# Masked attention layer on one core: eleven exponential tiles, the mask in 1 KB pieces, and exponentials issued behind the value products

## The chip, the cores and the metric

The kernel runs on one core of a Trainium2 chip. The metric is the device time of the whole program in microseconds (us): 3736.42 us for the kernel before, the median of three runs (3731.55 to 3740.82).

A core has five engines that run side by side and wait for each other through semaphores: TensorE (PE in the profile; its weight loads are PEld), VectorE (DVE), ScalarE (ACT), GpSimd (POOL), and SyncE (SP), which here only issues transfers. Each engine works through its own queue of instructions. Transfers run on 16 DMA engines. Matrix products are written to PSUM, which has eight banks; everything else lives in SBUF, with 128 partitions.

## What is computed

One graph-attention layer over 8 batch entries of 2048 nodes with 256 channels and 8 heads of 32, with one adjacency matrix for all of them:

```python
qkv = jnp.einsum('fnc,ck->fnk', x, w_qkv)          # q, k, v: (F, N, H, D) each, F=8, N=2048, H=8, D=32
scores = jnp.einsum('fnhd,fmhd->fhnm', q, k) / jnp.sqrt(D)
scores = jnp.where((adj > 0)[None, None, :, :], scores, -1e9)
attn = jax.nn.softmax(scores, axis=-1)
t = jnp.einsum('fhnm,fmhd->fnhd', attn, v).reshape(F, N, C)
x1 = _layernorm(x + t, ln1_g, ln1_b)
h = jax.nn.relu(jnp.einsum('fnc,cd->fnd', x1, w1) + b1)
f_out = jnp.einsum('fnd,dc->fnc', h, w2) + b2
x2 = _layernorm(x1 + f_out, ln2_g, ln2_b)
return _layernorm(x + x2)                          # without weights
```

About one adjacency entry in 128 is set, but the kernel computes all scores and masks them.

## The kernel before

The work is cut into 1024 steps. A step `(f, qc, g, mb)` is one batch entry `f`, one quarter `qc` of the queries (512), one half `g` of the heads (4 heads) and one of 16 blocks `mb` of 128 keys. Sixteen steps with the same `(f, qc, g)` are called a group here, and a group with `g = 1` an odd one; an entry has eight groups.

The scores of a step lie in PSUM with the keys on the partitions. VectorE adds the mask (0, or -57344 where there is no edge) on the way to SBUF, in two halves, and ScalarE takes the exponential in place. The mask is kept as 8-bit floats, keys on the partitions, 8 KB per partition for a query quarter; two such tiles rotate.

```python
mkp = ctx.enter_context(tc.tile_pool(name="mkp", bufs=2))
ld = ctx.enter_context(tc.tile_pool(name="ld", bufs=LD))     # LD = 3 tiles for loads ("in")
pp = ctx.enter_context(tc.tile_pool(name="pp", bufs=10))     # "p": scores and exponentials, 8 KB per partition
...
def scores(item):
    f, qc, g, mb = item
    pt = PT[item] = pp.tile([P, 4, CH], F32, name="p")
    ps2 = [score_pair() for _ in range(2)]                   # two of three pairs of PSUM banks
    for half in (1, 0):
        for j in range(2):
            r = D * (2 * half + j)
            nc.tensor.matmul(ps2[half][:, j, :], KT[...][r:r + D, ...], QT[f, qc, g][r:r + D, :], start=True, stop=True)   # L223
    for half, ps in enumerate(ps2):
        nc.vector.tensor_tensor(pt[:, 2 * half:2 * half + 2, :], ps,
                                MK[f, qc][:, mb, None, :].to_broadcast([P, 2, CH]), ALU.add)      # L226
    nc.scalar.activation(pt, pt, AF.Exp, scale=1.0 / math.sqrt(D))                                # L228

def values(item):
    f, qc, g, mb = item
    if mb == 0:
        O[grp] = ps_x[state["side"]].tile(...)               # one of two PSUM banks, in turn by group
    for h in range(4):
        nc.tensor.matmul(O[grp][r:r + D, :], V[...], PT[item][:, h, :], start=(mb == 0), stop=(mb == LAST))   # L240
    if mb == LAST:
        OT[grp] = op.tile([P, CH], F32, name=f"oT{g}")
        nc.scalar.copy(OT[grp], O.pop(grp))                  # L244, frees the bank
```

The softmax's denominators need the sum of the 16 exponential tiles of a group. Two chains of four are added by DMA, one chain of seven on GpSimd, one tile is left alone, and the four sums go through TensorE at the group's end. A `p` tile is free again only when its sum is done:

```python
POOLED = (0, 3, 6, 8, 11, 13, 15)
MOVED = ((1, 4, 7, 10), (2, 5, 9, 12))
def add_up(item):
    for chain in MOVED:
        if mb in chain[1:]:
            nc.gpsimd.dma_start(PT[f, qc, g, chain[0]], PT.pop(item), accum_op=ALU.add)           # L257
    if mb in POOLED[1:]:
        nc.gpsimd.tensor_tensor(first, first, PT.pop(item), ALU.add)                              # L260
```

All other work (denominators, normalizations, the two dense layers, projections of the next entry, masks of the next quarter) is cut into small pieces that the program places between the steps, one PSUM bank's worth per step, in the bank that the current group doesn't use:

```python
LEAD = 2
for t, (f, qc, g, mb) in enumerate(items):
    if mb == 0 and t:
        state["side"] = 1 - state["side"]
    if f == 0 and g == 0 and mb == 0 and qc + 1 < NCK:
        start(t, mask_ahead(qc + 1), t + 28)
    if g == 1 and mb == 0 and (f or qc == NCK - 1) and ...:
        load_mask(f + (qc + 1) // NCK, (qc + 1) % NCK)
    ...
    if mb:
        advance(t, 1)                   # a piece of other work
    scores(items[t + LEAD])             # scores, mask and exponential of two steps ahead
    values(items[t])
    add_up(items[t])
```

The mask is made once, in the first entry: adjacency rows are loaded, VectorE turns them to 0 or -57344, TensorE transposes them, VectorE writes them as 8-bit floats, and the quarter goes to DRAM for the seven later entries. The first quarter is made before the first step, in four blocks; the others are made between the steps, four blocks `mc` each:

```python
def turn_mask(qc, mc):
    if mc == 0:
        MK[0, qc] = mkp.tile([P, MB, CH], F8, name="mask")
    yield INPUTS - 3                    # needs all three "in" tiles
    cv = take([P, TPC, CH], BF16)
    ts = [take([P, 2, CH], I32) for _ in range(2)]
    for half, t in enumerate(ts):
        nc.sync.dma_start(t, adj[...])                                                            # L121
        nc.vector.tensor_scalar(cv[:, 2 * half:2 * half + 2, :], t, 0.0, MASKED, op0=ALU.is_le, op1=ALU.mult)   # L122
        give(t)
        yield 1                         # go on a step later
    yield 1
    yield from mask_blocks(qc, mc, cv)  # two halves: 8 transposes (L136) and one minimum (L137) each
    give(cv)                            # after the last block of a quarter: MD[qc] <- MK[0, qc] (L140)

def begin():
    ...                                 # loads; first quarter of the mask; keys and values for g = 0
    for k in range(LEAD):
        scores(items[k])
    for c in range(NCK):
        yield from project(0, c, 1, rows[c][:, 2:4, :])      # keys and values for g = 1
```

Of the kernel before, what the change touches and what calls it, by code (L numbers as in the profile page):

```python
# [10 lines left out]
F32 = mybir.dt.float32  # L11
BF16 = mybir.dt.bfloat16
I32 = mybir.dt.int32
F8 = mybir.dt.float8e5
# [4 lines left out]
P = 128  # L19
H = 8  # L20
D = 32
# [32 lines left out]
def fast_path(ctx, tc, cst, x, adj, out, RS):  # L54
# [3 lines left out]

    LD = 3
    dp = ctx.enter_context(tc.tile_pool(name="dp", bufs=1, space=bass.MemoryType.DRAM))  # L60
    mkp = ctx.enter_context(tc.tile_pool(name="mkp", bufs=2))
    ld = ctx.enter_context(tc.tile_pool(name="ld", bufs=LD))
    kp = ctx.enter_context(tc.tile_pool(name="kp", bufs=2 * NCK + 2))
    qp = ctx.enter_context(tc.tile_pool(name="qp", bufs=2 * NCK + 2))
    vp = ctx.enter_context(tc.tile_pool(name="vp", bufs=2 * NCK + 2))
    pp = ctx.enter_context(tc.tile_pool(name="pp", bufs=10))
    work = ctx.enter_context(tc.tile_pool(name="work", bufs=1))
    yp = ctx.enter_context(tc.tile_pool(name="yp", bufs=2))
    op = ctx.enter_context(tc.tile_pool(name="op", bufs=1))
# [33 lines left out]
    def give(t):  # L103
        live[:] = [None if u is t else u for u in live]


    MD = dp.tile([NCK, P, MB * CH // 4], I32, name="md")
    MK = {}

    def words(mask):  # L110
        return mask.rearrange("p b q -> p (b q)").bitcast(I32)

    def turn_mask(qc, mc):
        if mc == 0:
            MK[0, qc] = mkp.tile([P, MB, CH], F8, name="mask")
        yield INPUTS - 3
        cv = take([P, TPC, CH], BF16)
        ts = [take([P, 2, CH], I32) for _ in range(2)]
        for half, t in enumerate(ts):
            q0 = qc * CH + half * 2 * P  # L120
            nc.sync.dma_start(t, adj[q0:q0 + 2 * P, mc * CH:(mc + 1) * CH].rearrange("(j p) m -> p j m", p=P))  # L121
            nc.vector.tensor_scalar(cv[:, 2 * half:2 * half + 2, :], t, 0.0, MASKED, op0=ALU.is_le, op1=ALU.mult)  # L122
            give(t)
            yield 1
        yield 1
        yield from mask_blocks(qc, mc, cv)
        give(cv)

    def mask_blocks(qc, mc, cv):
        for half in range(2):  # L130
            yield BANK
            ps = bank(BF16)
            for r in range(2):
                for j in range(TPC):
                    rr = 2 * half + r
                    nc.tensor.transpose(ps[:, r, j * P:(j + 1) * P], cv[:, j, rr * P:(rr + 1) * P], identb)  # L136
            nc.vector.tensor_tensor(MK[0, qc][:, mc * TPC + 2 * half:mc * TPC + 2 * half + 2, :], ps,  # L137
                                    cst["ones"][:, 0:1, None].to_broadcast([P, 2, CH]), ALU.min, saturate=False)
        if mc == NCK - 1:
            nc.sync.dma_start(MD[qc], words(MK[0, qc]))  # L140

    def load_mask(f, qc):
        MK[f, qc] = mkp.tile([P, MB, CH], F8, name="mask")
        nc.sync.dma_start(words(MK[f, qc]), MD[qc])


    QT, KT, V, XT = {}, {}, {}, {}
# [46 lines left out]
    def project(f, c, g, xT=None):  # L194
        if xT is None:
            xT = yield from reload(f, c)
            while len(KT) < (2 * f + g) * NCK + c:
                yield 1
        yield BANK
        KT[f, c, g] = channels(kp, "kT", xT, C + g * P)  # L200
        yield BANK
        ps = bank()
        for j in range(TPC):
            for a in range(2):
                nc.tensor.matmul(ps[:, j * P:(j + 1) * P], xT[:, a, j * P:(j + 1) * P],  # L205
                                 wqkv[:, a, 2 * C + g * P:2 * C + (g + 1) * P], start=(a == 0), stop=(a == 1))
        v = vp.tile([P, TPC, P], F32, name="v")
        nc.scalar.copy(v, ps.rearrange("p (j c) -> p j c", c=P))
        V[f, c, g] = v
        give(xT)  # L210
# [4 lines left out]
# [3 lines that stand above are left out]
        ps2 = [score_pair() for _ in range(2)]  # L218
# [4 lines that stand above are left out]
                nc.tensor.matmul(ps2[half][:, j, :], KT[f, mb // TPC, g][r:r + D, (mb % TPC) * P:(mb % TPC + 1) * P],  # L223
                                 QT[f, qc, g][r:r + D, :], start=True, stop=True)
        for half, ps in enumerate(ps2):
            nc.vector.tensor_tensor(pt[:, 2 * half:2 * half + 2, :], ps,  # L226
                                    MK[f, qc][:, mb, None, :].to_broadcast([P, 2, CH]), ALU.add)
        nc.scalar.activation(pt, pt, AF.Exp, scale=1.0 / math.sqrt(D))  # L228

    LAST = MB - 1  # L230

    def values(item):
        f, qc, g, mb = item
        grp = (f, qc, g)
        if mb == 0:
            i = state["side"]
            O[grp] = ps_x[i].tile([P, CH], F32, name=f"x{i}")
        for h in range(4):
            r = D * h
            nc.tensor.matmul(O[grp][r:r + D, :], V[f, mb // TPC, g][:, mb % TPC, r:r + D], PT[item][:, h, :],  # L240
                             start=(mb == 0), stop=(mb == LAST))
        if mb == LAST:
            OT[grp] = op.tile([P, CH], F32, name=f"oT{g}")
            nc.scalar.copy(OT[grp], O.pop(grp))  # L244
# [135 lines left out]
    def start(t, gen, due):  # L380
        fill.append([t, gen, 1, due])
        fill.sort(key=lambda e: e[3])
# [24 lines left out]
    def mask_ahead(qc):  # L407
        for mc in range(NCK):
            yield from turn_mask(qc, mc)
# [9 lines left out]
    def begin():  # L419
        flat = [pp.tile([P, 4, CH], F32, name="p").rearrange("p a q -> p (a q)") for _ in range(NCK + NCK // 2)]  # L420
        cols = [t.bitcast(I32).rearrange("p (j m) -> p j m", m=CH) for t in flat[:NCK]]
        cv = [t[:, i * 2 * CH:(i + 1) * 2 * CH].bitcast(BF16).rearrange("p (j m) -> p j m", m=CH)
              for t in flat[NCK:] for i in range(2)]
        rows = [pp.tile([P, 4, CH], F32, name="p") for _ in range(NCK)]
        for c in range(NCK):
            xc = rows[c][:, 0:2, :].rearrange("p a (b c) -> p (a b) c", c=C)
            nc.sync.dma_start(xc, x[0, c * CH:(c + 1) * CH, :].rearrange("(j p) c -> p j c", p=P))
            nc.sync.dma_start(cols[c], adj[0:CH, c * CH:(c + 1) * CH].rearrange("(j p) m -> p j m", p=P))
        MK[0, 0] = mkp.tile([P, MB, CH], F8, name="mask")
        for c in range(NCK):  # L430
            nc.vector.tensor_scalar(cv[c], cols[c], 0.0, MASKED, op0=ALU.is_le, op1=ALU.mult)
            xT = rows[c][:, 2:4, :]
            yield from turn_rows(rows[c][:, 0:2, :].rearrange("p a (b c) -> p (a b) c", c=C), xT)
            nc.sync.dma_start(XD[0][c], xT)
            XT[0, c] = xT
            if c == 0:
                yield from queries(0, 0, xT)
            yield from project(0, c, 0, xT)
            yield from mask_blocks(0, c, cv[c])
        for k in range(LEAD):  # L440
            scores(items[k])
        for c in range(NCK):
            yield from project(0, c, 1, rows[c][:, 2:4, :])

    def ask(f, c):
        xT = yield from reload(f, c)
        yield from queries(f, c, xT)
        give(xT)
# [2 lines left out]
        pass  # L451
    for c in range(1, NCK):
        start(0, ask(0, c), 2 * MB * c - LEAD - 1)
    state["side"] = 0
    for t, (f, qc, g, mb) in enumerate(items):
        if mb == 0 and t:
            state["side"] = 1 - state["side"]
        if f == 0 and g == 0 and mb == 0 and qc + 1 < NCK:
            start(t, mask_ahead(qc + 1), t + 28)
        if g == 1 and mb == 0 and (f or qc == NCK - 1) and (f + 1 < F or qc + 1 < NCK):  # L460
            load_mask(f + (qc + 1) // NCK, (qc + 1) % NCK)
        if f + 1 < F:
            for what, *which in NEXT.get((2 * qc + g, mb), []):
                due = t + MB // 2 if what is turn else items.index((f + 1, 0, which[1], which[0] * TPC)) - LEAD - 1
                start(t, what(f + 1, *which), due)
        if mb:
            advance(t, 1)
        if t + LEAD < len(items):
            nf, _, ng, nmb = items[t + LEAD]
            t0 = t  # L470
            while (nf, nmb // TPC, ng) not in V:
                advance(t0, 1)
                t0 += 1
            scores(items[t + LEAD])
        values(items[t])
        add_up(items[t])
        if mb == LAST:
            start(t + SUM, denominator(f, qc, g), t)
# [240 lines left out]
```

## Time and profile before

| | |
|---|---|
| median of three runs | 3736.42 us |
| span of the profiled execution | 3732.1 us |
| mean granted TensorE clock | 0.977 of full |
| bytes moved by DMA | 573.31 MB |
| `mask<-md`: loads of a mask quarter | 28 of 1024 KB, median 6.6 us to landing |
| `in<-in_adj_dram`: loads of adjacency rows in the loop | 24 of 512 KB, median 7.6 us to landing |
| `p<-p`: sums by DMA | 384 of 1024 KB, median 9.7 us to landing |

A group's row in the profile names the line of the kernel, the engine, the operation and its tiles, and then the count, the busy time and the mean duration in nanoseconds; behind the second bar stands how long the engine had been idle just before such instructions, and what released it. A busy share is an average over the run: the engine with the highest is not necessarily what each stretch waits for. A row of the timeline gives the start, the duration, the instruction, and in brackets the idle time before it with its releaser. The first entry runs from about 42 to 564 us, counted by its exponentials.

### The profile page before, as it was taken

To read this page: it belongs to the slowest core of one execution; us is meant where nothing else is said; L and a number is where in the kernel's file an instruction comes from. 1 tells how busy PE (TensorE), PEld (TensorE's weight loads), DVE (VectorE), ACT (ScalarE), POOL (GpSimd) and SP (SyncE) were. 2 spreads that over 40 slices of the span, in tenths; PEclk is the share of its full clock that TensorE was granted. 3 is DMA by queue.
4 is the path that set the end of the run, shared out by engine and by line. 5 is a ranking of instruction groups with operands and counts; after the bars stand their busy time and mean duration, and the time that the engine had idled before them with its cause. 6 is when DMAs were issued, how large, how long until landed. Compare 5 with 4: busy or idle time off the path is not lost. (4 is left out here: it accounts for less than half of the span.)

```text
span 3732.1 us, 53786 instructions
## 1 busy us (share of the span) xinstructions
PE 3241.8 (87%) x22020; PEld 1038.8 (28%) x22020; DVE 2760.8 (74%) x3203; ACT 2411.0 (65%) x1921; POOL 2599.1 (70%) x1363
## 2 busy tenths in 40 slices
PE   7877888899988899889998899889898889988884
PEld 4222223222322233222332223222232222322221
DVE  4777766877688766788677777777768877688883
ACT  3554555766667666766666776666666676677663
POOL 2555666777677775877667785777777777687775
PEclk9998999999999999999999999999999999999997
DMA  6766675776766775776766776676676676676664
GB/s 185 175 142 152 146 175 117 168 162 142 173 150 145 158 171 145 169 153 154 169 138 151 163 172 158 140 165 154 147 175 141 148 171 152 154 164 140 139 134 86
DMA packets 113774, 573.31 MB, mean 154 GB/s; under 512 B 10833, under 2 KB 27729, under 8 KB 60273
## 3 DMA queue, kind: packets, MB, share of 16 engines
q0 software_dynamic: 64848, 436.90, 58.1%
q1 hardware_dynamic: 47856, 131.61, 10.0%
q8 instruction: 174, 2.85, 0.3%
q10 hardware_dynamic: 816, 1.31, 0.1%
q14 instruction: 80, 0.65, 0.0%
HBM read 129.37 MB, written 37.75 MB: 45 GB/s over the span
## 5 line engine op out<-in xcount | busy, mean ns | idle before, releaser
L226 DVE TENSOR_TENSOR p<-s,mask 128x1024 f32<-128x1024 f32 x2048 | 2410.3, 1219 | 753.8 <-PE s L223 480.0
L228 ACT ACTIVATE p<-p 128x2048 f32<-128x2048 f32 x1024 | 1957.1, 1911 | 1232.9 <-DVE p L226 916.2
L260 POOL TENSOR_TENSOR p<-p 128x2048 f32<-128x2048 f32 x384 | 1835.9, 4810 | 653.6 <-ACT p L228 645.0
L223 PE MATMUL s<-qT,kT 32*128 32x512 f32 x8192 | 1193.2, 652 | 232.5 <-DVE p L226 231.0
L240 PE MATMUL x<-p,v 128*32 128x512 f32 x8192 | 1112.2, 616 | 0.0
L257 POOL DMA_DIRECT2D p<-p x384 | 382.7, 1018 | 351.2 <-ACT p L228 138.9
L223 PEld LDWEIGHTS s<-qT,kT 32*128 32x128 f32 x8192 | 325.3, 186 | 853.6 <-DVE p L226 695.6
L240 PEld LDWEIGHTS x<-p,v 128*32 128x32 f32 x8192 | 162.3, 108 | 795.2 <-issue 645.1
L180 PE MATMUL x<-in,wqkv 128*128 128x512 f32 x472 | 234.6, 620 | 23.1 <-ACT oT L244 10.2
L278 ACT ACTIVATE y<-y,nb,rs 128x256 f32<-128x256 f32 x384 | 224.9, 589 | 38.0 <-POOL nb L275 38.0
L294 PE MATMUL x<-p,ones 128*32 128x512 f32 x2048 | 246.3, 599 | 1.8 <-DVE y L364 0.9
L267 DVE BATCH_NORM_STATS2 st<-y 128x6 f32<-128x256 f32 x384 | 160.1, 417 | 27.1 <-DMA y<-in_x_dram 27.1
L362 PE MATMUL x<-w2s,hT 128*128 128x256 f32 x512 | 127.6, 392 | 45.7 <-ACT oT L244 42.3
L352 PE MATMUL x<-turned,w1s 128*128 128x512 f32 x256 | 128.8, 626 | 20.8 <-ACT hT L353 19.5
L180 PEld LDWEIGHTS x<-in,wqkv 128*128 128x128 f32 x472 | 80.3, 190 | 186.1 <-issue 69.8
L362 PEld LDWEIGHTS x<-w2s,hT 128*128 128x128 f32 x512 | 92.1, 190 | 112.0 <-ACT oT L244 68.6
L205 PE MATMUL x<-wqkv,in 128*128 128x128 f32 x896 | 114.9, 282 | 6.4 <-ACT kT L182 6.3
L205 PEld LDWEIGHTS x<-wqkv,in 128*128 128x128 f32 x896 | 104.2, 192 | 55.0 <-ACT kT L182 34.0
L364 DVE TENSOR_TENSOR y<-x,y 128x512 f32<-128x512 f32 x64 | 44.3, 692 | 94.9 <-PE x L362 94.7
L294 PEld LDWEIGHTS x<-p,ones 128*32 128x32 f32 x2048 | 64.0, 111 | 165.8 <-issue 129.7
L272 POOL TENSOR_TENSOR rs<-rs,mhalf 128x4 f32<-128x4 f32 x96 | 99.3, 1035 | 8.0
L341 PE MATMUL x<-ident,y 128*128 128x128 f32 x256 | 48.0, 299 | 54.5 <-ACT turned L342 38.8
(87 smaller groups left out, 1427.1 us busy)
## 6 DMA issues: line engine op xcount, KB each, us to landing
p<-p POOLq DMA_DIRECT2D x384, 1024.0 KB, 9.7
y<-in_x_dram POOLq DMA_DIRECT2D x64, 512.0 KB, 6.1
in<-xd SPq DMA_DIRECT2D x59, 512.0 KB, 8.0
mask<-md SPq DMA_DIRECT2D x28, 1024.0 KB, 6.6
out_dram<-y SPq DMA_DIRECT2D x32, 512.0 KB, 3.0
in<-in_x_dram SPq DMA_DIRECT2D x28, 512.0 KB, 6.9
xd<-in SPq DMA_DIRECT2D x28, 512.0 KB, 10.0
in<-in_adj_dram SPq DMA_DIRECT2D x24, 512.0 KB, 7.6
```

Of the source, the lines that this page charges most:

```text
L180: nc.tensor.matmul(ps, wqkv[:, a, k0:k0 + P], xT[:, a, :], start=(a == 0), stop=(a == 1))
L205: nc.tensor.matmul(ps[:, j * P:(j + 1) * P], xT[:, a, j * P:(j + 1) * P], wqkv[:, a, 2 * C + g * P:2 * C + (g + 1) * P], start=(a == 0), s ...
L223: nc.tensor.matmul(ps2[half][:, j, :], KT[f, mb // TPC, g][r:r + D, (mb % TPC) * P:(mb % TPC + 1) * P], QT[f, qc, g][r:r + D, :], start=Tr ...
L226: nc.vector.tensor_tensor(pt[:, 2 * half:2 * half + 2, :], ps, MK[f, qc][:, mb, None, :].to_broadcast([P, 2, CH]), ALU.add)
L228: nc.scalar.activation(pt, pt, AF.Exp, scale=1.0 / math.sqrt(D))
L240: nc.tensor.matmul(O[grp][r:r + D, :], V[f, mb // TPC, g][:, mb % TPC, r:r + D], PT[item][:, h, :], start=(mb == 0), stop=(mb == LAST))
L257: nc.gpsimd.dma_start(PT[f, qc, g, chain[0]], PT.pop(item), accum_op=ALU.add)
L260: nc.gpsimd.tensor_tensor(first, first, PT.pop(item), ALU.add)
L267: nc.vector.bn_stats(st, t[:, j, :])
L278: nc.scalar.activation(t[:, j, :], t[:, j, :], AF.Identity, bias=nb[:, j:j + 1], scale=rs[:, j:j + 1])
L294: nc.tensor.matmul(ps[r:r + D, :], cst["ones"], term[:, h, :], start=(n == 0), stop=(n == 3))
L362: nc.tensor.matmul(ps[:, (j - jj) * C:(j - jj + 1) * C], hT[:, d, j * P:(j + 1) * P], w2s[:, d, :], start=(d == 0), stop=(d == 1))
```

## The change

Four things are changed together.

- Each quarter of the mask is kept as eight pieces of two key blocks, 1 KB per partition each, from a pool of nine pieces in place of two whole quarters. Pieces of the next quarter are loaded one by one during an odd group, each as a piece of the current quarter comes free. This gives room in SBUF.
- The room is used for an eleventh `p` tile.
- The second quarter of the mask is made at the start, with the first, in `p` tiles; the third and fourth are made in the loop, as before, but a block's adjacency rows are asked for two steps ahead of their conversion, and its masks are written into the tiles that held the rows and go to DRAM from there. In the first entry too, quarters two to four are then loaded back from DRAM.
- The exponential of a step is issued after the value products of the same turn of the loop, not right after its scores.

```diff
-    mkp = ctx.enter_context(tc.tile_pool(name="mkp", bufs=2))
+    mkp = ctx.enter_context(tc.tile_pool(name="mkp", bufs=MB // 2 + 1))
-    pp = ctx.enter_context(tc.tile_pool(name="pp", bufs=10))
+    pp = ctx.enter_context(tc.tile_pool(name="pp", bufs=11))
@@ turn_mask @@
-    MD = dp.tile([NCK, P, MB * CH // 4], I32, name="md")
+    MD = dp.tile([NCK, MB // 2, P, 2 * CH // 4], I32, name="md")
+    made, coming = set(), deque()
+    def mask_piece(t, qc, k):
+        MK[t, qc, k] = mkp.tile([P, 2, CH], F8, name="mask")
+        return MK[t, qc, k]
...
             nc.sync.dma_start(t, adj[q0:q0 + 2 * P, mc * CH:(mc + 1) * CH].rearrange("(j p) m -> p j m", p=P))
+        yield 2
+        for half, t in enumerate(ts):
             nc.vector.tensor_scalar(cv[:, 2 * half:2 * half + 2, :], t, 0.0, MASKED, op0=ALU.is_le, op1=ALU.mult)
+        yield 1
+        yield from mask_blocks(qc, mc, cv, [... the tiles ts seen as 8-bit floats ...])
+        for t in ts:
             give(t)
-            yield 1
-        yield 1
-        yield from mask_blocks(qc, mc, cv)
         give(cv)
@@ mask_blocks @@
-            nc.vector.tensor_tensor(MK[0, qc][:, mc * TPC + 2 * half:...], ps, ..., ALU.min, saturate=False)
-        if mc == NCK - 1:
-            nc.sync.dma_start(MD[qc], words(MK[0, qc]))
+            k = 2 * mc + half
+            m = to[half] if to else mask_piece(0, qc, k)
+            nc.vector.tensor_tensor(m, ps, ..., ALU.min, saturate=False)
+            nc.sync.dma_start(MD[qc, k], words(m))
+            made.add((qc, k))
+    def load_mask(f, qc, k):
+        nc.sync.dma_start(words(mask_piece(f, qc, k)), MD[qc, k])
@@ scores @@
-        nc.scalar.activation(pt, pt, AF.Exp, scale=1.0 / math.sqrt(D))
+    def exponentials(item):
+        nc.scalar.activation(PT[item], PT[item], AF.Exp, scale=1.0 / math.sqrt(D))
@@ begin @@
         for k in range(LEAD):
             scores(items[k])
+            exponentials(items[k])
         for c in range(NCK):
+            t = pp.tile([P, 4, CH], F32, name="p").rearrange("p a q -> p (a q)")
+            col = t.bitcast(I32).rearrange("p (j m) -> p j m", m=CH)
+            nc.sync.dma_start(col, adj[CH:2 * CH, c * CH:(c + 1) * CH].rearrange("(j p) m -> p j m", p=P))
+            nc.vector.tensor_scalar(cv[c], col, 0.0, MASKED, op0=ALU.is_le, op1=ALU.mult)
             yield from project(0, c, 1, rows[c][:, 2:4, :])
+            yield from mask_blocks(1, c, cv[c], [... the tile t seen as 8-bit floats ...])
@@ loop @@
+        if c > 1:
+            start(MB * (c - 1), mask_ahead(c), 2 * MB * c - MB // 2)
...
-        if f == 0 and g == 0 and mb == 0 and qc + 1 < NCK:
-            start(t, mask_ahead(qc + 1), t + 28)
-        if g == 1 and mb == 0 and (f or qc == NCK - 1) and (f + 1 < F or qc + 1 < NCK):
-            load_mask(f + (qc + 1) // NCK, (qc + 1) % NCK)
+        if g == 1 and mb % 2 and (f + 1 < F or qc + 1 < NCK):
+            coming.append((f + (qc + 1) // NCK, (qc + 1) % NCK, mb // 2))
+        while coming and coming[0][1:] in made:
+            load_mask(*coming.popleft())
...
             scores(items[t + LEAD])
         values(items[t])
+        if t + LEAD < len(items):
+            exponentials(items[t + LEAD])
         add_up(items[t])
```

## The prediction

> **What bounds the kernel now.** I read the page first, then the waits, then single stages of the timeline, then stages cut at the start of every 16th exponential. The page's busy line and its group rows:
>
> ```profile
> PE 3241.8 (87%) x22020; PEld 1038.8 (28%) x22020; DVE 2760.8 (74%) x3203; ACT 2411.0 (65%) x1921; POOL 2599.1 (70%) x1363
> L226 DVE TENSOR_TENSOR p<-s,mask 128x1024 f32<-128x1024 f32 x2048 | 2410.3, 1219 | 753.8 <-PE s L223 480.0
> L260 POOL TENSOR_TENSOR p<-p 128x2048 f32<-128x2048 f32 x384 | 1835.9, 4810 | 653.6 <-ACT p L228 645.0
> ```
>
> The kernel has 1024 steps, 16 to a group (one query quarter, four heads), 8 groups to a batch entry. TensorE is the busiest engine. The stages (columns: window, length, then busy time of PE, PEld, DVE, ACT, POOL, then clock, DMA share, GB/s) show how tightly:
>
> ```profile
> 42.40:118.50 76.10, 56.38 (x376) 21.77 (x376) 50.86 (x46) 35.07 (x25) 29.87 (x12) 0.87 0.58 140
> 176.40:632.60 456.20, 373.70 (x2507) 121.77 (x2507) 329.96 (x356) 257.06 (x199) 275.52 (x136) 0.94 0.66 151
> 1077.30:1133.70 56.40, 49.91 (x324) 14.62 (x316) 41.56 (x51) 39.86 (x35) 49.60 (x26) 0.97 0.74 159
> 1470.60:1914.60 444.00, 397.53 (x2702) 125.53 (x2705) 333.89 (x390) 298.88 (x238) 321.29 (x168) 0.99 0.70 156
> ```
>
> A later batch entry (last row) takes 444.0 us with TensorE busy 397.5: 46.5 us idle, everything else beside it. The first entry is different: its first group takes 76.1 us, and the seven groups from its third on (the last of them already the second entry's) take 456.2 us with 82.5 us of TensorE idle and a clock of 0.94. So there are two kinds of time to win: small TensorE waits that come back in each entry, and waits of the first entry alone. The waits (total us, times, longest) name the first kind:
>
> ```profile
> PE s L223 <- DVE p L226: 231.0, 333, 8.7
> PE x L362 <- ACT oT L244: 42.3, 29, 1.5
> PE x L180 <- ACT oT L244: 10.2, 7, 1.5
> PE x L136 <- ACT oT L244: 4.5, 3, 1.5
> ```
>
> Three places of the timeline show what stands behind them. First, a group's end:
>
> ```profile
> 1028.20 1.06 PE L240 MATMUL x<-p,v 128*32 128x512 f32 x8
> 1030.74 1.06 PE L240 MATMUL x<-p,v 128*32 128x512 f32 x8
> 1030.83 1.91 ACT L228 ACTIVATE p<-p 128x2048 f32<-128x2048 f32 x1 [2.21 <-DVE p L226]
> 1032.65 0.57 ACT L244 COPY oT<-x 128x512 f32<-128x512 f32 x1
> 1033.27 2.00 PE L362 MATMUL x<-w2s,hT 128*128 128x256 f32 x8 [1.46 <-ACT oT L244]
> ```
>
> The group's last value product ends at 1029.26. The copy of its result waits in ScalarE's queue behind an exponential that starts only at 1030.83, and TensorE, which needs that bank, waits 1.46 us. Second, the start of an odd group; third, a mask block of the first entry:
>
> ```profile
> 1078.90 2.36 DVE L226 TENSOR_TENSOR p<-s,mask 128x1024 f32<-128x1024 f32 x2 [1.26 <-DMA p<-p]
> 1080.18 1.80 PE L223 MATMUL s<-qT,kT 32*128 32x512 f32 x8 [2.03 <-DVE p L226]
> ...
> 83.60 0.69 DVE L122 TENSOR_SCALAR in<-in 128x1024 bf16<-128x1024 int32 x1 [7.85 <-DMA in<-in_adj_dram]
> 85.48 2.09 PE L223 MATMUL s<-qT,kT 32*128 32x512 f32 x8 [8.67 <-DVE p L226]
> ```
>
> At 1078.90 the masked add waits for one of ten `p` tiles still in the summing chain, and TensorE waits behind it. At 83.60 VectorE stands 7.85 us at a conversion whose adjacency rows have just been asked for, and TensorE 8.67 us.
>
> **What the Trainium skill says.** "TensorE: Matmul & The Clock Gate", section "Architectural detail", has ScalarE and VectorE as strict FIFO; the copy at 1032.65 and the conversion at 83.60 agree. The same page, "What's actually happening", says that an idle window of about 3.4 us halves the clock. Here scores that normally take 1.14 us take 2.09 after the 8.67 us wait, and 1.80 after one of only 2.03 us. "DMA: Bandwidth & Descriptors", "Specifications", wants at least 512 B per transfer; the new pieces are 1 KB per partition, so I don't expect them to be slow, though no run here has such pieces yet.
>
> **Part 1, the exponential behind the value products.** Instruction by instruction, the order on ScalarE differs in the loop by one thing: at each group's end the copy of the result stands ahead of the next exponential. It needs the value products (ended 1029.26) and the exponential before (1026.71 + 1.91 = 1028.62), so it can end near 1029.9, before TensorE asks at 1031.8 and before the next exponential's input is there at 1030.8. The three waits go: 42.3 + 10.2 + 4.5 = 57.0 us in 39 places. TensorE is the bound there (2.00 us of side products, scores right after without waiting), so most should reach the end. I take seven eighths: **50 us**.
>
> **Part 2, the eleventh tile.** Mask pieces (nine of 1 KB for two of 8 KB per partition) make room for it. VectorE's waits on the moved sums are 25.8 us in 19 places over the whole run, and 18.2 in 16 between 1027 and 3630 us. Most stand, as at 1078.90, at an odd group's second step, when GpSimd has the tail's work besides (49.60 busy of 56.40 us in the third window). One more tile lets VectorE run one step (2.5 us or more) ahead, more than the typical 1.3 us. I take 18 us. The clock in that window was 0.97: 0.03 x 56.4 = 1.7 us lost after the stall. Some ten groups look so; counting half a loss each, 10 x 0.85 = 8. Since part 1 brings the steps closer together while GpSimd doesn't get faster, I take off 4: **22 us**.
>
> **Part 3, mask blocks in the loop.** Twelve blocks become eight. VectorE's waits before conversions: 35.6 us in 8, plus lengthened conversions (24 take 32.0 us; at the median 0.685 they would take 16.4, so 15.6 more): 51 us. The first group has 9.3 + 2.0 = 11 of them, the other eight blocks 40, or 5 per block. After the change the loads are asked for two steps ahead of the conversions. But a block's loads reuse tiles that the block before writes its mask from, so where blocks follow each other they start only when that block's last transpose is masked; counted in the built order, six of eight do, with two steps of adds between. A load lands after 8.2 us (median from 42 to 577 us), plus 0.8 to issue two; two steps hide 5.5 to 6: 3 us per block, 18, and 2 for the others. So 40 - 20 = 20 us. The clock's deficit, 0.06 x 456 = 27 us, may halve; two thirds of that count: 9. Gain **29 us**.
>
> **Part 4, the second quarter at the start.** Its four blocks now stand between the first two exponentials and the loop, and the SyncE queue issues a block's load behind the mask writes of the block before. So they run in series: 1 MB load 5.5 us (an estimate: 4.9 was measured for writing a mask of 1 MB, 3.7 the shortest of 512 KB), conversion 1.23, transposes 0.8, two minima 2.44, issues 1: 11 us, four times 44. They start at 39.2, so step 2's add moves from 57.8 to about 84: 26 us lost. The first group then has no blocks: before, 60.7 us from step 2's add to exponential 16; after, 14 x 2.55 = 36, query products 6, slow clock 4: 46, or 15 back. Net **-11 us**.
>
> **Part 5, mask pieces in the loop.** 248 small loads in place of 28 large ones, issued in odd groups only, each behind the add that frees its buffer, a dozen steps ahead of use. The bytes are about the same: 0 us.
>
> Sum: 50 + 22 + 29 - 11 = 90; 3736 - 90 = **3646 us**.
>
> **Rivals.** (a) GpSimd becomes the bound: it has 49.6 of 56.4 us in odd groups. Then closer steps only lengthen the tile waits, parts 1 and 2 give half, and the time is near 3685. Against it: even groups leave it 18 us idle (31.14 busy in the 48.7 us from 1133.7), and the eleventh tile spans the gap. (b) The serial start costs more and the blocks still stall, since loads took up to 16.2 us: parts 3 and 4 together give -15 in place of +18, 3679. (c) The block stalls vanish, TensorE keeps its clock everywhere and all 57 us count: 3605. (d) The small pieces hold up the SyncE queue and delay the reloads of x; for it speaks that the queue is in order, against it the dozen steps of lead; it would put 20 to 60 us back.
>
> **Range and chances.** From (c) to (a) and (b) with something of (d): 3605 to 3690. The 2% line is 3661.7, only 16 us above my value, against an uncertainty of some 30 us: faster by over 2% with 0.67, within 2% with 0.32, slower 0.01.
>
> **What would show it.** Right: no wait of TensorE for the result's copy; even groups of later entries 1.5 us shorter (48.7 to 47.2); odd groups without the wait for `p<-p` at their second step; a later entry near 435 us; step 2's add near 84 us; conversions that wait about 3 us. Wrong: the copy's wait replaced by one of scores on adds of the same size, new VectorE waits on GpSimd, adds waiting for mask pieces, or conversions that wait as long as before.

## The result, and the profile after

The changed kernel takes 3651.55 us (median of 4 runs, 3651.02 to 3655.0) against 3733.99 us before; the ratio is 0.978, 95% interval 0.9762 to 0.9798. That is 82 us less, close to the 90 predicted. The sum held, but not each of its terms: parts 1 and 2 gave more than predicted, part 3 gave next to nothing.

The page's busy line and the two group rows that answer to those of before:

```profile
PE 3215.7 (88%) x22020; PEld 1037.2 (28%) x22020; DVE 2757.1 (76%) x3199; ACT 2413.6 (66%) x1921; POOL 2601.5 (71%) x1363
L233 DVE TENSOR_TENSOR p<-s,mask 128x1024 f32<-128x1024 f32 x2048 | 2408.9, 1218 | 696.4 <-PE s L230 404.8
L269 POOL TENSOR_TENSOR p<-p 128x2048 f32<-128x2048 f32 x384 | 1852.7, 4872 | 575.3 <-ACT p L237 573.3
```

The work is the same (22020 matmuls). TensorE is busy 26 us less; by the trace's clock record its time at half clock fell by 34 us over the run (172 to 138), which accounts for at most 17 of them. The stages, with the columns of the stages shown before:

```profile
42.10:131.30 89.20, 72.45 (x424) 29.34 (x424) 51.92 (x44) 38.04 (x31) 28.20 (x12) 0.89 0.59 148
186.20:631.00 444.80, 363.84 (x2496) 118.86 (x2500) 321.86 (x352) 257.27 (x198) 266.03 (x133) 0.93 0.67 153
1063.80:1118.00 54.20, 48.49 (x324) 14.58 (x324) 41.53 (x51) 39.79 (x35) 47.55 (x25) 1.00 0.82 177
1461.30:1895.30 434.00, 397.20 (x2723) 126.72 (x2723) 336.10 (x393) 301.12 (x241) 324.35 (x168) 1.00 0.73 160
```

Rows 3 and 4, an odd group and a whole entry, went from 56.4 to 54.2 and from 444.0 to 434.0 us, and their clock is now full. Row 2, the first entry's groups with mask blocks, has hardly moved (456.2 to 444.8), and its clock is as low as before. The waits (total us, times, longest):

```profile
PE s L230 <- DVE p L233: 171.8, 348, 5.5
PEld x L249 <- ACT oT L253: 46.3, 61, 0.8
DVE in L127 <- DMA in<-in_adj_dram: 41.4, 8, 9.0
PE x L143 <- DVE in L127: 44.7, 8, 8.7
ACT p L237 <- ACT oT L253: 9.5, 22, 0.8
```

TensorE's three waits for the result's copy are gone. Only the weight load (PEld) and the exponential still wait for it, 0.8 us at most. But the wait before conversions grew from 35.6 to 41.4 us, for 16 conversions where there were 24. Two of the three places of the timeline, a group's end and an odd group's second step:

```profile
1016.37 1.06 PE L249 MATMUL x<-p,v 128*32 128x512 f32 x8
...
1017.50 0.59 ACT L253 COPY oT<-x 128x512 f32<-128x512 f32 x1 [0.57 <-PE x L249]
...
1019.00 1.91 ACT L237 ACTIVATE p<-p 128x2048 f32<-128x2048 f32 x1 [0.91 <-DVE p L233]
...
1066.75 2.35 DVE L233 TENSOR_TENSOR p<-s,mask 128x1024 f32<-128x1024 f32 x2 [0.19 <-PE s L230]
...
1068.02 1.14 PE L230 MATMUL s<-qT,kT 32*128 32x512 f32 x8 [0.41 <-DVE p L233]
```

The copy now follows the group's last value product at once (1017.43 to 1017.50), ahead of the exponential. The add at 1066.75 waits for scores, not for a `p` tile, and the scores after it take 1.14 us instead of 1.80. The third place, the worst mask block after the change:

```profile
228.61 1.68 SPq L124 DMA_DIRECT2D in<-in_adj_dram  x2
...
237.98 0.69 DVE L127 TENSOR_SCALAR in<-in 128x1024 bf16<-128x1024 int32 x1 [8.96 <-DMA in<-in_adj_dram]
...
246.91 0.69 DVE L127 TENSOR_SCALAR in<-in 128x1024 bf16<-128x1024 int32 x1 [8.24 <-DMA in<-in_adj_dram]
...
248.79 2.09 PE L230 MATMUL s<-qT,kT 32*128 32x512 f32 x8 [0.31 <-DVE p L233]
250.04 1.91 ACT L237 ACTIVATE p<-p 128x2048 f32<-128x2048 f32 x1 [18.95 <-DVE p L233]
```

The rows are asked for at 228.61, and VectorE stands 8.96 and then 8.24 us for them; the scores that follow run at half clock (2.09 us).

### The profile page after: what moved, and what is told of

Read it like the earlier page. It is cut to its first block, busy times and chain, and to the rows that moved or that the text cites. A ratio compares the mean times of both kernels' runs of the same rounds, so it can differ in the third digit from the quotient of the medians.

```text
span 3649.4 us, 54415 instructions
## 1 busy us (share of the span) xinstructions
PE 3215.7 (88%) x22020; PEld 1037.2 (28%) x22020; DVE 2757.1 (76%) x3199; ACT 2413.6 (66%) x1921; POOL 2601.5 (71%) x1363
## 5 line engine op out<-in xcount | busy, mean ns | idle before, releaser
L230 PE MATMUL s<-qT,kT 32*128 32x512 f32 x8192 | 1179.6, 644 | 173.4 <-DVE p L233 171.8
L249 PE MATMUL x<-p,v 128*32 128x512 f32 x8192 | 1097.4, 608 | 0.0
L212 PEld LDWEIGHTS x<-wqkv,in 128*128 128x128 f32 x896 | 104.2, 191 | 55.9 <-ACT kT L189 38.3
L378 POOL TENSOR_TENSOR y<-y,be2r 128x1024 f32<-128x1024 f32 x32 | 93.3, 2916 | 0.2
```

## Where the time went, by stages

Stages are cut at starts of exponentials, numbered from 0. The third column is the time from exponential 144 to 1023. "Half clock" is the time at half clock between exponentials 32 and 144, and in the third stage, from the trace's clock record. "Stops" is VectorE's wait before the loop's conversions plus their lengthening over 0.69 us, with the number of blocks (two conversions each).

```
us                               0-32   32-144  144-1023  half clock   stops, blocks
before                           134.0  456.2   3025.5    58.0, 51.2   51.2, 12
after                            144.1  444.8   2941.6    58.0,  6.8   54.1,  8
before, exponential late         141.5  451.5   2971.5    54.6, 30.7   59.7, 12
after, exponential early         147.5  452.5   2989.0    54.6,  3.4   53.4,  8
after, ten tiles                 145.9  445.6   2967.9    58.0, 23.9   55.3,  8
mask parts only                  145.7  455.3   3020.9    68.3, 30.7   55.1,  8
after, second quarter in loop    146.8  469.5   2940.5    78.5, 10.2   84.5, 12
after, loads five ahead          147.8  421.4   2942.5    41.3,  3.4   28.7,  8
after, 2nd quarter's rows early  126.8  448.7   2942.1    64.9,  6.8   56.3,  8
after, conversion strided        149.7  471.1   2942.6    81.9,  3.4   83.7,  8
ten tiles, masks in own tiles    145.4  441.5   2965.1    58.0, 17.1   51.8,  8
after, both mendings             128.4  427.0   2942.7    44.1,  3.4   29.3,  8
the same, conversion on ScalarE  120.1  423.3   2945.6    41.0, 10.2    -     8
after, no masks in the loop      139.6  375.6   2942.6     0.0,  6.8    -     0
```

From before to after: +10.1, -11.4 and -83.8; with -0.3 ahead of the first exponential and +2.6 behind the start of the last that is the -82.8 between the two profiled spans. The prediction had about 72 x 879/1024 = 62 for the third column, +11 for the first, and for the second -29 from part 3 alone. So the late entries gave 22 us more than expected, and the blocks gave next to nothing.

The second stage hides that the first entry itself became longer: exponentials 0 to 128 take 540.1 us instead of 521.2. The stage is shorter only because its last group, the second entry's first, went from 69.0 to 48.8 us. In the kernel before, that group still makes 93 matmuls of its entry's projections; in the kernel after it makes 16, and the others are done by then.

The start also differs from one measurement to the next. Three of the runs below (loads five ahead, conversion strided, no masks in the loop) change nothing ahead of exponential 16, yet it starts at 135.1, 137.2 and 139.0 us, against 131.3 in the kernel after. A difference from 3651.55 us that was not measured together with it is therefore uncertain by some 4 to 8 us. The first four runs below were measured together, and so can be compared with each other.

## The experiments

**Part 1 alone, on the kernel before.**

```diff
         nc.vector.tensor_tensor(pt[...], ps, MK[f, qc]..., ALU.add)
-        nc.scalar.activation(pt, pt, AF.Exp, scale=1.0 / math.sqrt(D))
+    def exponentials(item): ...          # called in the loop behind values(items[t])
```

> The kernel before with one part of the change: each exponential issued behind the value products of its turn (ten tiles, whole mask quarters as before). Theory A (TensorE bound, the parts add up): the 57.0 us of waits for the result's copy go, the time falls by 45 to 60 us, to about 3682. Rival B (GpSimd's summing chain bounds the odd groups, so a faster even group only lengthens the waits for tiles): a fall of 25 to 30 us, to about 3707, with VectorE's waits for p<-p growing at the odd groups' second step.

3684.03 us, ratio 0.9851 (0.9831 to 0.987), 56.8 us less than before in the same comparison. The 57.0 us of copy waits are won in full, not at seven eighths. 54.0 us come in the third stage, which had 48.1 us of these waits; its time at half clock fell too, from 51.2 to 30.7 us.

**Part 1 undone, on the kernel after** (the call of `exponentials` directly behind `scores`).

> The changed kernel with the exponential put back right behind its scores. Theory A: the copy's waits return (near 57 us in 39 places), time about 3651 + 50 = 3702. Rival B (the eleventh tile carries most of the gain and hides the waits): under 3675.

3715.39 us, 0.9938 (0.9921 to 0.9955): 63.8 us more than the kernel after. The waits are back, 55.6 us in 38 places:

```profile
PE x L371 <- ACT oT L253: 43.8, 30, 1.5
PE x L187 <- ACT oT L253: 11.8, 8, 1.5
```

48.2 us of them lie in the third stage, which is 47.4 us longer, and its half clock does not return (3.4 us). So with eleven tiles the waits alone account for part 1; the half clock goes with the tile. Of the 63.8 us some 10 lie ahead of exponential 32 and behind the start of the last one, outside the stages that the waits fill. The two measurements bracket part 1 at 57 to 64 us.

**Part 2 undone.**

```diff
-    pp = ctx.enter_context(tc.tile_pool(name="pp", bufs=11))
+    pp = ctx.enter_context(tc.tile_pool(name="pp", bufs=10))
```

> The changed kernel with ten tiles p in place of eleven. Theory A: waits for p<-p return at the odd groups' second step, together with half-clock windows after them; 22 to 35 us more, about 3680. Rival B (tile waits and copy waits are the same wait seen twice): 45 us or more, above 3696. If neither, and the tile was not needed: within 8 us of 3651.

3682.62 us, 0.9854 (0.9836 to 0.9871): 31.1 us more. The wait that the tile removes, first with ten tiles, then with eleven:

```profile
DVE p L233 <- DMA p<-p: 20.2, 22, 1.4
```

```profile
DVE p L233 <- DMA p<-p: 1.9, 4, 0.8
```

18 us of waits go, and 17.1 us of half clock in the third stage (23.9 to 6.8), worth up to half of that, 8.5. Together up to 27, and the third stage differs by 26.3 us. The other 5 of the 31.1 lie at the start (exponential 16 at 137.0 us instead of 131.3).

**The mask parts alone** (the kernel after with ten tiles and the early exponential: parts 3, 4 and 5 without 1 and 2).

> The changed kernel with ten tiles and the exponential in its old place: the mask pieces, the second quarter at the start and the earlier loads alone. Theory A: a later batch entry as long as in the kernel before (444 us), the first entry about equal too, since conversions still wait; 3725 to 3740. Rival C (mask pieces cost or gain something in the later entries): an entry differs from 444 us by more than 2 us, in seven entries more than 14 us in all.

3745.97 us, 1.001 (1.0003 to 1.0017): 5 us *more* than before, where the prediction had 29 - 11 = 18 less. Against this run, measured with it, the late exponential alone gives 63.4 us (ten tiles, 3682.62) and the eleventh tile alone 30.6 (exponential early, 3715.39); with the tile the third stage's half clock falls from 30.7 to 3.4 us. The parts add up: 56.8 + 31.1 - 5.1 = 82.8, and 82.4 was measured; that they agree so closely is chance, given the uncertainty of the start. So the overestimate lies in the mask parts, and the 1 KB pieces as such were no large gain either (the third stage is 4.6 us shorter than before).

**Loads five steps ahead of the conversion.**

```diff
-        yield 2
+        yield 5
         for half, t in enumerate(ts):
             nc.vector.tensor_scalar(cv[...], t, 0.0, MASKED, op0=ALU.is_le, op1=ALU.mult)
```

> The changed kernel with a mask block's rows asked for five steps ahead of their conversion in place of two. Theory L (in the first entry's loop the conversions wait since two steps do not cover a load, which took up to 23.9 us from issue to landing): the 41 us of conversions waiting for rows fall below 12, the time falls by 30 to 45 us, to about 3613. Rival Q (blocks that take three steps longer hold the three load tiles longer and push the next entry's rows and projections into the first entry's end): the waits go, but the time falls by less than 12 us or rises.

3639.69 us, 0.9742 (0.9726 to 0.9759): 12 us less than after. The waits fell as expected:

```profile
DVE in L127 <- DMA in<-in_adj_dram: 6.4, 1, 6.4
PE x L143 <- DVE in L127: 23.0, 8, 6.8
```

41.4 became 6.4 here (8.1 with the waits that this view puts elsewhere), yet TensorE still waits 23.0 us for conversions, because these now take longer: 20.6 us in all beyond 0.69 each, instead of 12.7. So the two-step lead was one cause, but the time fell by less than the 30 to 45 us of theory L. In the second stage the gain is 23.4 us; exponential 16, ahead of which nothing changed, starts 3.9 us later. And rival Q came true in part: groups 2 to 4 of the first entry (counted from 0) take 175.7 us instead of 214.6, but its last group and the next entry's first take 132.0 instead of 111.5, with 773 matmuls instead of 718, because projections of the next entry slid back behind the blocks. Why conversions take longer, the strided conversion below asks.

**The second quarter's rows asked for while the first quarter is made.**

```diff
+        def ask_rows(c): ...             # p tile and load of the second quarter's rows
         for c in range(NCK):
+            if c < NCK - 1:
+                ask_rows(c)
             nc.vector.tensor_scalar(cv[c], cols[c], 0.0, MASKED, op0=ALU.is_le, op1=ALU.mult)
```

> The changed kernel with the rows of the second mask quarter asked for while the first quarter is made (three of four blocks; the fourth after the first projection), not block by block. Theory S (the four blocks at the start run in series because each load stands behind the mask writes of the block before): step 2's add comes about 20 us earlier, near 63 us in place of about 84, and the time falls by 18 to 24 us, to about 3630. Rival: the loads were not the limit (TensorE at half clock or VectorE's minima are), under 8 us.

3636.84 us, 0.9731 (0.9714 to 0.9747): 15 us less than after, short of the 18 to 24 expected. Exponential 2 starts at 70.4 us instead of 85.6. The serial loads of part 4 were a real cost, and most of it was avoidable.

**No mask blocks in the loop.** Masks of the third and fourth quarter are left out, and their pieces read from the second quarter's place: those queries get another mask, and everything else does the same work.

> The changed kernel without making the third and fourth quarter of the mask: their pieces are loaded from the second quarter's place, so the scores of those queries get another mask. It measures what the eight mask blocks in the loop cost in all. Theory L: their work alone is small (TensorE 8 x 1.2 us, VectorE 8 x 3.8 us) and their waits large (54 us at VectorE), so 55 to 75 us less, about 3587. Rival: the waits lie beside other work, under 35 us less.

3578.52 us, 0.9577 (0.9561 to 0.9593): 73 us less, or 9.1 per block. The half clock of the second stage, 58.0 us, is gone altogether (0.0): the blocks cause all of it, for up to 29 of the 73.

**The conversion in strided order,** meant to make it independent of GpSimd.

```diff
-            nc.vector.tensor_scalar(cv[:, 2 * half:2 * half + 2, :], t, ...)
+            nc.vector.tensor_scalar(cv[...].rearrange("p j m -> p m j"), t.rearrange("p j m -> p m j"), ...)
```

> The changed kernel with the conversions of the loop walking their tiles in a strided order (same result), which should keep them from the port that VectorE shares with GpSimd. Theory P (five of sixteen conversions took 1.6 to 4.7 us in place of 0.68 because a GpSimd sum held that port: each ends 0.7 us after the sum's end): every conversion takes the same, an estimated 1.1 to 1.4 us, none is lengthened, and the time changes by less than 8 us. Rival: they were waiting for rows, and long ones remain.

3682.75 us, 0.9855 (0.9838 to 0.9871): 31 us more than after, and the aim was missed twice. A conversion took 2.75 to 3.04 us, and four were still lengthened. This is the first of them, two conversions in one line:

```profile
174.67 4.53 POOL L269 TENSOR_TENSOR p<-p 128x2048 f32<-128x2048 f32 x1 [3.10 <-ACT p L237]
175.04 9.26 DVE L127 TENSOR_SCALAR in<-in 128x1024 bf16<-128x1024 int32 x2
```

The same place of the kernel after:

```profile
168.71 4.52 POOL L269 TENSOR_TENSOR p<-p 128x2048 f32<-128x2048 f32 x1 [3.09 <-ACT p L237]
169.08 5.31 DVE L127 TENSOR_SCALAR in<-in 128x1024 bf16<-128x1024 int32 x2
173.84 0.28 PE L143 MATMUL x<-identb,in 128*128 128x128 bf16 x2 [3.62 <-DVE in L127]
```

GpSimd's sum runs from 168.71 to 173.23. The first conversion begins at 169.08 and ends at 173.79, 0.56 us after the sum. In strided order the sum ends at 179.20 and the conversion at 181.79, 2.59 later. Each time it is about the conversion's own length after the end of GpSimd's operation: it stands until GpSimd is done. The other long conversions of the kernel after (4.27, 3.48, 2.09 and 1.64 us) end 0.55 to 0.57 us after a GpSimd operation in the same way (the expectation's 0.7 us was too much). The page "SBUF — State Buffer" of the Trainium skill, section "SBUF: two separate sides", says of the port pair that VectorE and GpSimd share that whichever starts first holds it for its whole instruction, and the other blocks; on VectorE's side this concerns operations in a two-port mode or with two SBUF inputs. The trace agrees for the conversion (0.56 us after the sum), and shows the same for the strided form (2.59 us); in which mode either ran, no run here shows. The run also tells what longer conversions cost: the sixteen take 57.8 us in all instead of 23.7, 34 more on VectorE; the second stage is 26 us longer, the run 31.

**Both mendings,** loads five ahead and the second quarter's rows early.

> The kernel after with both mendings: the second quarter's rows asked for while the first quarter is made, and the loop's rows asked for five steps ahead of their conversion. If the two concern separate stretches (the start, before exponential 16; the blocks, between exponentials 16 and 144), the gains add: -12 and -15 from 3651.6, so 3625 us (3619 to 3631), with exponential 2 near 70 us and exponential 16 to 144 near 478 us. Rival: part of the one is given back by the other, because TensorE's clock or GpSimd's sums set the next groups anyway: 3632 to 3640.

3622.24 us, 0.9709 (0.969 to 0.9729). The gains add up (3625 expected).

**Part 4 undone alone:** the second quarter's four blocks back among the first group's steps.

```diff
-            t = pp.tile(...); ... nc.vector.tensor_scalar(cv[c], col, ...)      # begin
-            yield from mask_blocks(1, c, cv[c], [...])
-        if c > 1:
-            start(MB * (c - 1), mask_ahead(c), 2 * MB * c - MB // 2)
+        start(32 if c == 2 else MB * (c - 1), mask_ahead(c), 2 * MB * c - MB // 2)
-        while coming and coming[0][1:] in made:
+        while coming and coming[0][1:] in made and (coming[0][1] != 1 or (1, MB // 2 - 1) in made):
```

> Part 4 undone alone: the kernel after, but with the second quarter's four blocks back among the first group's steps, with loads two steps ahead; the third quarter's blocks start 16 steps later than in the kernel after, so that they don't mix with these. Theory S (the serial start costs what the stages show, about 10 to 13 us at exponential 16): exponential 2 near 60 us, exponential 16 near 118 to 120 and a total of 3639 to 3643. Rival C (crowding: blocks in the loop cost some 9 us each, so four blocks back in the loop cost more than the start saves): exponential 16 at 130 or later, a total of 3651 to 3665.

3682.24 us, 0.9866 (0.9849 to 0.9882): 30.7 us more than after, above the ranges of both theories, though exponential 16 (130.5 us) is where rival C had it. So part 4 does not cost 11 us; with part 3 in place it saves about 31. The start alone went as predicted: step 2's exponential 19.3 us behind the first one here and 43.5 after, 24 lost where 26 were expected. But up to exponential 32 the two are level (146.8 and 144.1), since the first group without blocks also takes up query and key products that otherwise fall into the second, and in the next stage the kernel after is 24.7 us ahead. The waits:

```profile
PE x L143 <- DVE in L127: 66.2, 14, 13.1
DVE in L127 <- DMA in<-in_adj_dram: 57.8, 12, 13.4
```

VectorE's stops are 84.5 us for twelve blocks, 33 more than before had for as many. Taking parts 1 and 2 (57 + 31 = 88) off the kernel before and adding 33 gives 3677; 3682 was measured. The edit is not quite pure: the third quarter's blocks start 16 steps later than in the kernel after.

**The conversion on ScalarE,** with both mendings.

```diff
-            nc.vector.tensor_scalar(cv[...], t, 0.0, MASKED, op0=ALU.is_le, op1=ALU.mult)
+            nc.scalar.activation(cv[...], t, AF.Copy, bias=MASKED, scale=-MASKED)
```

> The kernel with both mendings, and its sixteen conversions in the loop moved from VectorE to ScalarE (a copy with scale and bias, same values). Theory V (the groups with blocks are bound by the chain of TensorE and VectorE, so what leaves VectorE comes off the time at the rate of the strided conversions, 31 us for 37): off VectorE go 16 x 0.69 = 11 us, 19 us of lengthening beside GpSimd's sums and 8 us of waits, 38 in all, so 25 to 32 us less than the kernel with both mendings, near 3597. The ScalarE conversions should take about 1 us each (an exponential of twice the elements takes 1.91) and never be lengthened. Rival N (the time of these groups is set elsewhere, or the exponentials behind the conversions in ScalarE's queue take over the wait): 0 to 10 us less.

3609.91 us, 0.9669 (0.9653 to 0.9685): 12.3 us less than with both mendings, and the fastest version here that makes all masks. The tile's row (shortest, median, longest ns) and the waits:

```profile
L127 ACT ACTIVATE in<-in x16: 1037/1041/1056, 162.0 to 411.4; 128x1024 bf16<-128x1024 int32 x16
```

```profile
PE x L143 <- ACT in L127: 19.8, 10, 8.5
DVE in L146 <- ACT in L127: 15.3, 4, 10.2
ACT in L127 <- DMA in<-in_adj_dram: 7.7, 1, 7.7
```

No conversion is lengthened on ScalarE, as expected. But only 12 of the expected 25 to 32 us came: the transposes and minima now wait for ScalarE, where the conversion stands between exponentials. So the lengthening cost something, though not one for one.

**Masks written into tiles of their own,** with ten `p` tiles.

```diff
+    mst = ctx.enter_context(tc.tile_pool(name="mst", bufs=2))
-        yield from mask_blocks(qc, mc, cv, [... the tiles ts ...])
         for t in ts:
             give(t)
+        yield from mask_blocks(qc, mc, cv, [mst.tile([P, 2, CH], F8, name="turned") for _ in ts])
```

> To be compared with the kernel after with ten tiles (0.9854 of before, 43.4 us of waits before conversions). Here too there are ten tiles, and the loop's minima write their masks into two small tiles of their own (1 KB per partition each, in the room of the eleventh tile) instead of into the tiles that held the adjacency rows, so that a block's rows no longer wait for the landing of the block before's mask write. Lead and order are unchanged: rows asked for two steps ahead, behind the mask writes in SyncE's queue. Theory T (the reuse of the tiles makes the loads late): waits before conversions fall below 25 us and the time by 11 to 19 us, to a ratio of 0.980 to 0.982. Rival Z (two steps are simply too short for a load, and the issue behind the mask writes in SyncE's queue costs the same as the reuse): waits stay at 35 to 45 us, ratio 0.984 to 0.986.

3680.58 us, 0.9849 (0.9827 to 0.987), no different from ten tiles without it (0.9854). The waits are still there:

```profile
DVE in L128 <- DMA in<-in_adj_dram: 38.3, 8, 9.8
```

43.4 became 38.3. The reuse of the row tiles, to which the prediction had given the remaining stalls, is not what holds the blocks up. The lead of two steps is, as the run with five shows.

## Why the prediction was right, and where it was not

**Part 1: mechanism right, size low.** The copy ends as worked out (1018.09 in the group shown, ahead of the exponential), and the waits are gone. Of 57.0 us seven eighths were taken; 57 to 64 came. The waits reach the end in full: 48 us of them in the third stage make it 47.4 us longer with eleven tiles and 53 to 54 with ten. With eleven tiles the clock adds nothing (3.4 and 6.8 us at half clock).

**Part 2: mechanism right, size low.** 22 us predicted, 26 (third stage) to 31 measured. The waits (18) and the clock (8) were of the right size, 18 and up to 8.5. The 4 us taken off for a GpSimd that doesn't keep up were not needed: an odd group is 2.2 us shorter with GpSimd busy 47.55 of 54.20 us, so rival (a) falls. A later entry takes 434.0 us where 435 was foretold, and the third group of each later entry, 48.7 to 48.8 us before, takes 47.1 to 47.4 where 47.2 was foretold.

**Part 3: wrong, and this is the failed step.** The prediction said "3 us per block" and that the clock's deficit "may halve". Measured were 41.4 us of waits in eight blocks, 5.2 each, 12.7 us of lengthening, 1.6 each, and 58.0 us at half clock, the same as before. Three things stand behind it.
- The load was taken at 8.2 us, a median. After the change the median is 5.9, but the range goes from 4.0 to 23.9, and two steps of 2.5 us cover only short ones. The row of the second load of 228.61, and the queues while it was under way (packets, MB, share of the 16 engines):

```profile
q0 software_dynamic: 401, 2.89, 78.6%
q1 hardware_dynamic: 544, 1.05, 16.5%
...
in<-in_adj_dram SPq DMA_DIRECT2D x1, 512.0 KB, 17.8
```

  GpSimd's accumulating sums (the first queue) hold 78.6% of the DMA engines; the row's load, in the second, took 17.8 us. That the one slows the other is read from the shares and was not tested.
- 15.6 us of lengthened conversions of before were counted as waits for loads. They are waits for GpSimd, which an earlier load cannot shorten: with loads five ahead they grew from 12.7 to 20.6.
- The gain was put at half of the stops, though the blocks now stop VectorE for 6.8 us each instead of 4.3 (54.1 / 8 against 51.2 / 12). Fewer blocks times longer stops came to about the same, 54 us.

**Part 4: start right, worth wrong.** Step 2's add moved as foretold (exponential 2 from 60.2 to 85.6 us), and the first stage grew by 10.1 us against 11 predicted. But what four blocks cost in the loop in their new form was not asked: about 9 us each, 36 in all. Undoing the part costs 31 us, 25 of them in the second stage. The prediction charged these blocks the price that they had in the kernel before. If the parts add, part 3 applied to all twelve blocks would make the kernel slower by some 36 us (5 + 31); this alone was not run.

**Part 5: right.** The 248 pieces land after 5.6 us at the median, no add waits for one, and the third stage with the pieces and without parts 1 and 2 is even 4.6 us shorter than before. Rival (d) falls.

**Rival (b)** described the mask parts best: blocks still stall, the start costs what was feared, together nearly nothing (it had -15, measured -5). The total came out right because parts 1 and 2 gave 88 us instead of 72, while parts 3 and 4 gave -5 instead of 18: an error of 16 against one of 23. That the two errors nearly cancel is luck.

**What stays open.** The first stage differs by up to 8 us between kernels whose code there is nearly the same (134.0 before, 141.5 with the late exponential), so terms under 10 us in it are not settled. And of the 9.1 us per block, up to 3.6 is clock and 6.8 stops, which overlap; how they divide was not separated. Of the 31 us for part 4, some may belong to the third quarter's later start.

## What to carry to other kernels

A load that is issued ahead must be covered for its slow landings, not for its median: when an in-order engine waits for the load, every late one stops the whole pipeline. Before counting a long instruction as a wait for its input, look at where it ends. One that always ends just behind another engine's operation is waiting for that engine. And price a part that moves work by what the work costs in its *new* surroundings, since a second part of the same change may have made it dearer.

## What the runs showed of the hardware that was not expected

- A conversion of 128x1024 int32 to bf16 on VectorE, 0.69 us alone, took up to 4.70 us in the kernel after beside a GpSimd sum of 4.5 us, and ended about 0.56 us behind it; masked adds, which read PSUM and one SBUF operand, kept their mean of 1.218 us throughout. On ScalarE the same conversion took 1.04 us (1.037 to 1.056), with GpSimd working beside it.
- Walking the same data in the order "p m j" made the conversion four times as long (2.75 us against 0.69), and it was still held up.
- Loads of 512 KB from DRAM landed after 4.0 to 23.9 us in the same kernel.
- The later entries' time at half clock went with the eleventh tile. With it, VectorE's waits for a `p` tile fell from 20.9 us (24 times, 1.8 us at most) to 2.3, and half clock from 30.7 to 3.4 us with the exponential early; with it late, from 23.9 to 6.8. TensorE's waits for the copy were as frequent and as short (33 of about 1.5 us in these entries), but putting them back did not bring half clock back (3.4 us). The length of a single wait thus does not tell which ones slow the clock. Each of these figures is from one profile, and the mask parts alone, which touch neither wait, also show 30.7 us against 51.2 before; but the mean granted clock of all runs agrees, 0.979 to 0.981 with the tile (kernel after, and the same with the exponential early), 0.975 to 0.979 with ten (the same two).
